# An 8-bit feed-forward block in a multi-stage kernel: the first map made feature-major, convolution taps applied behind it

## The chip, the cores and the metric

The kernel runs on one core of a Trainium2 chip. A core has five engines that run their own instruction streams: PE (TensorE, matrix products and transposes; "PEld" is its weight load), DVE (VectorE), ACT (ScalarE), POOL (GpSimd), and SP (SyncE), which here issues DMAs. The metric is the device time of one execution in microseconds (us). It is told as the median of several executions; one further execution is profiled, and all durations in the text come from that one.

## The reference

The reference is a long residual network over x, of shape (4, 512, 128): four layers, each with a cross attention and a feed-forward block. The change concerns the feed-forward block of the second layer, whose weights and inputs are rounded to few levels (a "bit linear" map):

```python
def act_quant(x):                       # per token, 8 bit
    scale = 127.0 / clip(max(abs(x), -1), 1e-5)
    return clip(round(x * scale), -128, 127) / scale

def weight_quant(w):                    # one scale per matrix, values -1, 0, 1
    scale = 1.0 / clip(mean(abs(w)), 1e-5)
    return clip(round(w * scale), -1, 1) / scale

h = bit_linear(x, w1)                   # (4, 512, 128) -> (4, 512, 512)
h = depthwise_conv1d(h, conv_w) + conv_b   # over tokens, 3 taps, zero padding, one filter per feature
h = silu(h)
x = x + bit_linear(h, w2)               # (4, 512, 512) -> (4, 512, 128)
```

The input x of the block is layer-normalized before. Written out for token t and feature f, the value in front of silu is c0[f] u[t-1, f] + c1[f] u[t, f] + c2[f] u[t+1, f] + b[f], where u is the first map's output and u outside of the row of 512 tokens is zero.

## The kernel before

**Stages.** The whole program is a sequence of stages. Most of them, and all that matter here, are written as a plan: pieces of work with the pieces they wait for, the buffers they take and use, and a planned cost on each engine that could do them (PE, V for DVE, S for ACT, G for POOL, Q for SP; costs in units of 10 ns). `Plan.run` (L191) is a list scheduler: it takes the ready piece that can start first, with the longest remaining path breaking ties, and issues it to the engine on which it would end first. The result is a fixed order of instructions on each engine; on the chip each engine runs its own order and waits in it. So an instruction that waits holds everything that stands behind it on its engine. PSUM has eight banks, which the plan hands out; buffers in SBUF come in rings of two or three.

The stages that the change touches, with their place in the profiled execution:

- *Expert stage of layer 0* (`first_part`, second plan, 176 to 322 us). Eight experts, one after the other: load the sorted tokens (`xe`, L1051), turn them, first map with silu (L1571 to L1578), second map (L1589), weighting on DVE (`ye`, L1134), and an indirect store per 128 tokens from POOL (L1020). Beside it, as filler, the plan prepares what later stages need: `bit_weights` (L1168) and `window_tables` (L1389), whose Exp runs at L1422.
- *Middle stage* (`middle_part`, 322 to 522 us). One plan holds the second layer's cross attention (`L686` to `L840`), the 8-bit block (`bit_ffn`, L1257), the third layer's window attention (L1439), and a normalization with a turn (L1614 to L1628) that hands the rows to the local transformer. All of it runs over four rows (batch entries b, 512 tokens each); the plan interleaves the rows. The rows' tensors x appear in the order of the program as x_79, x_81, x_83, x_85 for rows 0 to 3.
- *Local transformer* (522 to 2184 us), whose first weight loads SP issues at L1739.

**The 8-bit block.** For each row b: normalization (`norm`: moments on DVE at L536 and L538, 1/sigma on POOL at L546 and L547, then applied on DVE or POOL at L552); rounding to 8 bits by adding and subtracting a large constant (`scales` L1268 to L1271, `lift` L1278, `settle` L1283, either on DVE or POOL); four transposes (L1298) and a copy to `xqT`, the row with features on partitions and 512 tokens plus a zero column at either end (`ends`, L1292).

Then for each of the row's four token tiles (128 tokens): `hidden` (L1311) makes all 512 features of the tile in one PSUM bank by four products into one accumulation. A first one with a bfloat16 matrix of three rows adds the bias, and three fp32 products add one tap each; a tap is a shift of `xqT` by one column, with its own copy of the weights:

```python
t = hb.view(128, FF)
e.matmul(t, first[0:32], cb[0:32], start=True, stop=False)
for j in range(3):
    e.matmul(t, xqT.t[:, 128*tt + j : 128*tt + j + 128], w1T[:, j], start=False, stop=(j == 2))
```

The tile then has tokens on partitions. Silu is tanh on ACT (L1322) and one pass on DVE (L1325); the second rounding is per token (`scales` L1335 to L1338 on DVE, `inverse` L1341 on POOL, `lift` L1345 or L1347, `settle` L1352 or L1354); four bfloat16 transposes (L1364), a copy (`hqT`), the second map (L1371) and the residual add (L1377).

**The weights.** `bit_weights` loads w1, w2, the taps `cw` and the bias `cb`; rounds both matrices to -1, 0, 1 (`ternary`: L1206 to L1218); makes for each tap j a scaled copy of w1 (`tap`, L1232), turns it (L1236) and copies it to `w1T[:, j]`; and splits the bias, broadcast to all partitions, into three bfloat16 terms (`three_terms`, L316, called at L1195).

Of the kernel before, what the change touches and what calls it, by code (L numbers as in the profile page):

```python
# [239 lines left out]
def tile_kernel(ctx: ExitStack, tc: tile.TileContext, A: dict, out: bass.AP):  # L240
# [61 lines left out]
    def copy(e, dst, src):  # L302
        (e.copy if e is SC else e.tensor_copy)(dst, src)
# [864 lines left out]
    def bit_weights(plan, mp, wp):  # L1168

        w1, w2 = (wp.tile([128, NFC, 128], F32, name=f"bw{k}", bufs=1) for k in range(2))  # L1170
        cw = wp.tile([128, NFC, 3], F32, name="cw", bufs=1)
        cb = mp.tile([128, FF], BF16, name="cb")
        w1T = mp.tile([128, 3, FF], F32, name="w1T")
# [4 lines left out]
        row = plan.buf(wp, [128, FF], F32, "cbrow", 1)  # L1178

        def load(e):  # L1180
# [3 lines left out]
            e.dma_start(row.t, A["L1_ffn_conv_b"].partition_broadcast(128))  # L1184
# [5 lines left out]
        loaded = plan.add(load, takes=[row], Q=200)  # L1190
        done = [plan.add(magics, G=30, V=20)]
        for k in range(4):
            def terms(e, k=k):
                at = slice(128 * k, 128 * k + 128)
                three_terms(cb[:, at], row.t[:, at], wp, [128, 128], e)  # L1195

            done.append(plan.add(terms, [loaded], uses=[row], V=120))
# [27 lines left out]
        t1, t2 = ternary(w1, m1), ternary(w2, out_scale)  # L1225

        for j in range(3):
            bank, wj = plan.bank(), plan.buf(wp, [128, NFC, D], F32, "wj")

            def tap(e, j=j, wj=wj):  # L1230
                for c in range(NFC):
                    e.tensor_scalar(wj.t[:, c], w1[:, c], m1, cw[:, c, j : j + 1], ALU.mult, ALU.mult)  # L1232

            def flip(e, bank=bank, wj=wj):
                for c in range(NFC):
                    e.transpose(bank.view(128, NFC, 128)[:, c], wj.t[:, c], ident)  # L1236

            def out(e, j=j, bank=bank):
                copy(e, w1T[:, j], bank.view(128, FF))

            p = plan.add(tap, [t1], takes=[wj], V=112)
            p = plan.add(flip, [p], takes=[bank], uses=[wj], PE=54)
            done.append(plan.add(out, [p], uses=[bank], S=59, V=69))
# [11 lines left out]
        return done, w1T, w2T, cb, out_scale, magic  # L1255

    def bit_ffn(plan, wp, weights, start):  # L1257
        done, w1T, w2T, cb, out_scale, magic = weights
        last = []
        for b in range(B):  # L1260
# [29 lines left out]
            xqT, bank = plan.buf(wp, [128, S + 2], F32, "xqT"), plan.bank()  # L1290

            def ends(e, xqT=xqT):  # L1292
                e.memset(xqT.t[:, 0:1], 0.0)
                e.memset(xqT.t[:, S + 1 : S + 2], 0.0)
# [944 lines left out]
```

## Time and profile before

| | |
|---|---|
| median of three runs | 2434.31 us (2431.93 to 2436.33) |
| the profiled execution, its own time | 2475.2 us |
| its span in the profile | 2473.4 us |
| mean granted clock of PE | 0.956 |
| PE busy | 2242.8 us, 91% of the span |
| DVE busy | 1745.4 us, 71% |
| POOL busy | 1383.7 us, 56% |
| ACT busy | 1291.9 us, 52% |

Of the first map in the profile: the products with taps (L1315) are 96 records of 592 ns (an fp32 product leaves two), the bias products (L1313) 16 of 385 ns, the tanh (L1322) 16 of 597 ns, the pass behind it (L1325) 16 of 678 ns.

How to read the views that follow: the busy time by stretch gives, for a stretch of time, its length, the busy time of PE, PEld, DVE, ACT and POOL (with the number of instructions), the granted clock of PE as a share of full speed, and the load of the DMA engines. The chain of waits goes back from the last instruction, at each step to what released it; each of its lines has a start, the time that the chain spends there, the engine, the tensor written and the line. A timeline row has a start, a duration, the engine, the line, the operation, out<-in with shapes, and in brackets how long the engine was idle before it and what released it. Matmuls overlap: a record's duration is longer than the distance between two in a row, so sums over PE are made from the chain.

### The profile page before, as it was taken

The numbers are of one execution on the slowest core, as the hardware profiler recorded it, in microseconds if no ns is written. First come the engines' busy times: TensorE is split into PE (matmuls) and PEld (weight loads), VectorE is DVE, ScalarE is ACT, GpSimd is POOL, SyncE is SP. The second block draws the span as 40 slices with busy tenths as digits, with TensorE's granted clock in tenths as the row PEclk, the third lists the DMA queues.
The fourth block names the chain that finished last, engine by engine and source line by source line (L and its number), as shares of the span: only waits on it lengthen the run. The fifth ranks groups of instructions, "written<-read, shape, count | busy, mean of one in ns | idle before, by whom it ended". The sixth has DMA issues, their size and how long they took to land.

```text
span 2473.4 us, 86733 instructions
## 1 busy us (share of the span) xinstructions
PE 2242.8 (91%) x37341; PEld 1478.8 (60%) x37341; DVE 1745.4 (71%) x3818; ACT 1291.9 (52%) x2379; POOL 1383.7 (56%) x1948
## 2 busy tenths in 40 slices
PE   7959879968999999999999999999999999988686
PEld 3527644536666666666666666666666666644364
DVE  5626355757788888877887888888888888765522
ACT  3523225535666556666666666566666666533232
POOL 2242232446667666676667667766667666532433
PEclk9969989989999999999999999999999999989688
DMA  7210110015411121111211121111211111120022
GB/s 161 87 42 21 36 42 2 1 51 102 118 29 35 31 60 50 26 35 35 70 35 31 33 79 32 30 35 29 76 35 32 30 35 34 30 78 10 23 75 82
DMA packets 134297, 116.14 MB, mean 47 GB/s; under 512 B 29505, under 2 KB 102700, under 8 KB 133916
## 3 DMA queue, kind: packets, MB, share of 16 engines
q1 hardware_dynamic: 128373, 102.81, 16.0%
q0 software_dynamic: 4608, 7.35, 0.9%
q8 instruction: 296, 4.85, 0.8%
q14 instruction: 85, 0.70, 0.1%
q10 hardware_dynamic: 935, 0.43, 0.1%
HBM read 42.84 MB, written 21.52 MB: 26 GB/s over the span
## 4 chain that ended last, share of the span: by engine, by line
PE 71%; DVE 15%; issue 4%; DMA 3%; POOL 3%; ACT 2%; another core or an unknown queue 1%; SPq 1%; POOLq 0%; DVEq 0%; ACTq 0%
PE ps_tr L585 12%; PE ps_mm L1786 11%; PE ps_av L1948 6%; PE ps_av L1924 5%; PE ps_tr L1863 5%; PE ps_sc L1893 4%; DVE xn L523 3%; PE ps_sc L1994 2%; PE ps_sc L2006 2%; PE ps_sc L1983 2%; PE ps L776 2%; PE ps L1315 2%; PE ps L1687 2%; PE ps L785 2%; PE ps L1571 1%
## 5 line engine op out<-in xcount | busy, mean ns | idle before, releaser
L1809 POOL TENSOR_TENSOR rc<-rc,rs 128x512 f32<-128x512 f32 x384 | 489.8, 1276 | 382.7 <-DVE rs L1799 324.0
L1786 PE MATMUL ps_mm<-wqk,y 128*128 128x512 f32 x768 | 398.0, 601 | 10.4 <-DVE rs L1799 7.0
L1828 POOL TENSOR_TENSOR rc<-rc,rn_y 128x512 f32<-128x512 f32 x384 | 388.6, 1044 | 7.5
L1796 DVE TENSOR_TENSOR rc<-ps_mm,tabs 128x512 f32<-128x512 f32 x384 | 262.3, 683 | 139.1 <-ACT sq L1788 124.7
L1788 ACT ACTIVATE sq<-ps_mm 128x512 f32<-128x512 f32 x384 | 231.2, 603 | 167.0 <-PE ps_mm L1786 119.2
L1799 DVE TENSOR_TENSOR rs<-ps_mm,tabs 128x512 f32<-128x512 f32 x384 | 261.2, 680 | 0.3
L1808 DVE TENSOR_REDUCE ss<-sq 128x8 f32<-128x512 f32 x384 | 259.3, 675 | 0.0
L585 PE MATMUL ps_tr<-cst,rc 128*128 128x128 f32 x1536 | 211.7, 281 | 7.3 <-issue 4.1
L1924 PEld LDWEIGHTS ps_av<-v,PT 64*32 64x32 f32 x12288 | 138.4, 105 | 124.8 <-PE ps_tr L585 54.9
L1948 PE MATMUL ps_av<-aT,wo 128*128 128x128 f32 x1536 | 198.0, 281 | 4.3 <-issue 4.2
L1948 PEld LDWEIGHTS ps_av<-aT,wo 128*128 128x128 f32 x1536 | 179.5, 191 | 13.5 <-issue 4.6
L585 PEld LDWEIGHTS ps_tr<-cst,rc 128*128 128x128 f32 x1536 | 166.0, 142 | 27.9 <-issue 6.0
L1924 PE MATMUL ps_av<-v,PT 64*32 64x65 f32 x12288 | 170.3, 225 | 5.1 <-DVE attn L1934 1.1
L1893 PE MATMUL ps_sc<-kT,qT 64*32 64x64 f32 x12288 | 146.0, 224 | 25.3 <-issue 24.6
L1020 POOL DMA_INDIRECT back<-ye,to x80 | 78.0, 975 | 160.3 <-DVE ye L1134 117.7
L1786 PEld LDWEIGHTS ps_mm<-wqk,y 128*128 128x128 f32 x768 | 124.9, 193 | 60.5 <-issue 49.7
L1893 PEld LDWEIGHTS ps_sc<-kT,qT 64*32 64x32 f32 x12288 | 139.6, 105 | 35.1 <-issue 28.9
L766 ACT ACTIVATE P<-ps,deltaT 77x512 f32<-77x512 f32 x192 | 115.0, 684 | 69.2 <-PE ps L760 61.8
L1909 ACT ACTIVATE P<-P 128x1024 f32<-128x1024 f32 x96 | 101.5, 1057 | 90.9 <-DVE P L1904 90.9
L1820 ACT ACTIVATE rn_y<-ss 128x32 f32<-128x32 f32 x96 | 22.0, 229 | 236.6 <-POOL ss L1819 236.6
L1840 ACT COPY qT<-ps_tr 128x512 f32<-128x512 f32 x192 | 103.3, 589 | 75.4 <-PE ps_tr L585 75.1
L1840 ACT COPY kT<-ps_tr 128x512 f32<-128x512 f32 x192 | 103.4, 590 | 66.3 <-PE ps_tr L585 66.2
(410 smaller groups left out, 4414.3 us busy)
## 6 DMA issues: line engine op xcount, KB each, us to landing
v<-v SPq DMA_DIRECT2D x432, 65.0 KB
v<-v SPq DMA_DIRECT2D x96, 195.0 KB
wqk<-in_L_ffn_Wqkv_dram SPq DMA_DIRECT2D x24, 256.0 KB
sent<-xn SPq DMA_DIRECT2D x2, 2210.0 KB
xe<-sent SPq DMA_DIRECT2D x16, 260.0 KB
back<-xn SPq DMA_DIRECT2D x2, 2048.0 KB
raw<-in_L_ffn_W_dram SPq DMA_DIRECT2D x8, 512.0 KB
yb<-back SPq DMA_DIRECT2D x16, 256.0 KB
```

What stands on the lines that cost most here:

```text
L585: PE.transpose(t[:, i], src[:, i], ident)
L1786: PE.matmul(t, lhs, T.w[2 * kind + c], start=True, stop=True)
L1788: SC.activation(sq, t, AF.Square)
L1796: V.tensor_tensor(a, t, bc(T.tabs[:, 2 * kind, tt], [128, 8, LD], 1), ALU.mult)
L1799: V.tensor_tensor(r.rearrange("p h (x d) -> p h x d", x=2), t.rearrange("p h (x d) -> p h x d", x=2)[:, :, ::-1], bc(T.tabs[:, 2 * kind + ...
L1808: V.tensor_reduce(T.ss[:, kind, 8 * c : 8 * c + 8], sq, AX.X, ALU.add)
L1809: G.tensor_tensor(a, a, r, ALU.add)
L1828: G.tensor_tensor(a, a, bc(y[:, o : o + 8], [128, 8, LD], 2), ALU.mult)
L1840: SC.copy(t[:, 4 * c : 4 * c + 4, lead:], to_features(T.rot[kind, c].rearrange("p (k x) d -> p k (x d)", x=2)),)
L1893: PE.matmul(T.banks[32 * w : 32 * w + 32, z, k], T.qT[r, k, 32 * w : 32 * w + 32], T.kT[r, k, 32 * w : 32 * w + 64], start=False, stop=Tru ...
L1924: PE.matmul(T.means[32 * w : 32 * w + 32, x0, k], T.PT[r, 4 * g + k, 32 * w : 32 * w + 32], (T.v1 if w % 2 else T.v2)[r, x0, 4 * g + k], s ...
L1948: PE.matmul(t, T.wo[:, c], T.aT[:, c], start=(c == 0), stop=(c == 7))
```

## The change

In `bit_weights` the three scaled copies of w1 go, with their transposes, and one transposed copy of the rounded w1 takes their place (`flip1`, `out1`). The taps stay in a small tensor `cw` with features on partitions, multiplied once by the scale of w1 (`taps`). The bias is loaded with features on partitions, four values per partition, and isn't split any more.

In `bit_ffn` the first map runs with features on partitions: for each of four chunks of 128 features one product with all 512 tokens of the row (`product`). The result is read out of PSUM three times: once with the middle tap as scale and the bias as bias, on ACT (`own`, to `v`), and twice with an outer tap as scale, on ACT or DVE (`scaled`, to `n`). POOL adds the two neighbours in place, each one column out of step (`sides`); the missing neighbour at either end of the row is left out by the slices, so the zero columns of `xqT` and their memsets go. When all four chunks are done, `hidden` transposes the four chunks of a token tile into one PSUM bank, and all that follows is as before.

```diff
-        cw = wp.tile([128, NFC, 3], F32, name="cw", bufs=1)
-        cb = mp.tile([128, FF], BF16, name="cb")
-        w1T = mp.tile([128, 3, FF], F32, name="w1T")
+        cw = mp.tile([128, NFC, 3], F32, name="cw")
+        cb = mp.tile([128, NFC], F32, name="cb")
+        w1T = mp.tile([128, NFC, 128], F32, name="w1T")
...
-            e.dma_start(row.t, A["L1_ffn_conv_b"].partition_broadcast(128))
+            e.dma_start(cb, A["L1_ffn_conv_b"].rearrange("(c p) -> p c", p=128))
...
-        for k in range(4):
-            def terms(e, k=k):
-                at = slice(128 * k, 128 * k + 128)
-                three_terms(cb[:, at], row.t[:, at], wp, [128, 128], e)
-            done.append(plan.add(terms, [loaded], uses=[row], V=120))
...
-        for j in range(3):
-            bank, wj = plan.bank(), plan.buf(wp, [128, NFC, D], F32, "wj")
-            def tap(e, j=j, wj=wj):
-                for c in range(NFC):
-                    e.tensor_scalar(wj.t[:, c], w1[:, c], m1, cw[:, c, j : j + 1], ALU.mult, ALU.mult)
-            def flip(e, bank=bank, wj=wj):
-                for c in range(NFC):
-                    e.transpose(bank.view(128, NFC, 128)[:, c], wj.t[:, c], ident)
-            def out(e, j=j, bank=bank):
-                copy(e, w1T[:, j], bank.view(128, FF))
...
+        def taps(e):
+            e.tensor_scalar(cw, cw, m1, None, ALU.mult)
+        def flip1(e, bank=bank):
+            for c in range(NFC):
+                e.transpose(bank.view(128, NFC, 128)[:, c], w1[:, c], ident)
+        def out1(e, bank=bank):
+            copy(e, w1T, bank.view(128, NFC, 128))
...
-            xqT, bank = plan.buf(wp, [128, S + 2], F32, "xqT"), plan.bank()
-            def ends(e, xqT=xqT):
-                e.memset(xqT.t[:, 0:1], 0.0)
-                e.memset(xqT.t[:, S + 1 : S + 2], 0.0)
+            xqT, bank = plan.buf(wp, [128, S], F32, "xqT"), plan.bank()
...
+            v = plan.buf(wp, [128, NFC, S], F32, "bv")
+            mixed = []
+            for c in range(NFC):
+                ub, n = plan.bank(), plan.buf(wp, [128, 2, S], F32, "bn")
+                def product(e, c=c, ub=ub, xqT=xqT):
+                    e.matmul(ub.view(128, S), w1T[:, c], xqT.t, start=True, stop=True)
+                def own(e, c=c, ub=ub, v=v):
+                    e.activation(v.t[:, c], ub.view(128, S), AF.Identity,
+                                 scale=cw[:, c, 1:2], bias=cb[:, c : c + 1])
+                def scaled(e, c=c, ub=ub, n=n):
+                    for k in range(2):
+                        a, w = n.t[:, k], cw[:, c, 2 * k : 2 * k + 1]
+                        if e is SC:
+                            e.activation(a, ub.view(128, S), AF.Identity, scale=w)
+                        else:
+                            e.tensor_scalar(a, ub.view(128, S), w, None, ALU.mult)
+                def sides(e, c=c, n=n, v=v):
+                    d = v.t[:, c]
+                    e.tensor_tensor(d[:, 1:], d[:, 1:], n.t[:, 0, : S - 1], ALU.add)
+                    e.tensor_tensor(d[:, : S - 1], d[:, : S - 1], n.t[:, 1, 1:], ALU.add)
+                q = plan.add(product, [p] + done, takes=[ub], uses=[xqT], PE=88)
+                q = plan.add(own, [q], takes=[] if c else [v], uses=[ub] + ([v] if c else []), S=79)
+                r = plan.add(scaled, [q], takes=[n], uses=[ub], S=125, V=138)
+                mixed.append(plan.add(sides, [r], uses=[n, v], G=258))
...
-                    t = hb.view(128, FF)
-                    e.matmul(t, first[0:32], cb[0:32], start=True, stop=False)
-                    for j in range(3):
-                        e.matmul(t, xqT.t[:, 128 * tt + j : 128 * tt + j + 128], w1T[:, j],
-                                 start=False, stop=(j == 2))
+                    for c in range(NFC):
+                        e.transpose(hb.view(128, NFC, 128)[:, c],
+                                    v.t[:, c, 128 * tt : 128 * tt + 128], ident)
...
-                q = plan.add(hidden, [p] + done, takes=[hb], uses=[xqT], PE=285)
+                q = plan.add(hidden, mixed, takes=[hb], uses=[v], PE=58)
```

Since the plan decides the order, the new pieces and costs also move other pieces: in the middle stage rows 0 to 2 of the cross attention come earlier in PE's order than before, in the expert stage the loads of the window tables come ahead of the loads of the weights, and their Exp stands in the middle of an expert's silus instead of behind them.

## The prediction

> **What bounds the kernel now.** I read the page first (busy shares, slices), then the busy time by stretch around the changed stage, then the chain that ended last inside it, then the rows of single instructions. The change lies in two stages: the first expert stage (176 to 322 us), where the weights of the 8-bit block are prepared beside other work, and the middle stage (322 to 522), where the block runs between cross attention and window attention. The columns below are the stretch, its length, and busy time of PE, PEld, DVE, ACT and POOL, then PE's granted clock.
>
> ```profile
> 385.00:443.00 58.00, 57.66 (x730) 27.86 (x728) 32.69 (x92) 29.23 (x50) 16.86 (x32) 1.00 0.01 2
> 443.00:485.00 42.00, 41.69 (x188) 20.81 (x187) 30.48 (x104) 19.71 (x35) 18.42 (x34) 1.00 0.00 1
> 485.00:497.00 12.00, 9.08 (x79) 6.65 (x78) 11.08 (x47) 10.37 (x30) 3.60 (x8) 1.00 0.00 1
> 497.00:522.00 25.00, 17.15 (x102) 12.06 (x100) 17.59 (x79) 11.99 (x34) 7.66 (x11) 0.96 0.00 1
> ```
>
> From 385 to 485 PE is the bound, at full clock: 99.35 of 100 us. The other engines have room, POOL most. After 485 no engine is full; a chain of handoffs sets the pace. The chain shows what PE does:
>
> ```profile
> 442.73 0.32 PE ps L1313
> 443.05 2.77 PE ps L1315 x6
> 445.82 0.32 PE ps L1313
> 446.14 2.77 PE ps L1315 x6
> ...
> 519.89 1.26 PE ps L1618 x4
> 521.27 0.34 SPq L1739
> ```
>
> One token tile of the first map costs 0.32 (bias) + 2.77 (three taps) = 3.09 us, and sixteen of them 49.4 us. The last two lines say what the stage's end is worth: the weight loads of the next stage are issued right behind the last transposes of this one (SP's longest wait, 188.7 us, is for them). A microsecond saved at the end of the middle stage is therefore saved at the end of the kernel.
>
> **The middle stage, part by part.** PE: x6 in 2.77 us is three products, so one 128x512 product is 0.92 us; a row needs four, 16 x 0.92 = 14.8. Four fp32 transposes are 0.44 (the chain's L1298 x4), 16 x 0.44 = 7.1. PE falls from 49.4 to 21.9, **27.5 us less**. The two memsets (0.1 each) go for nothing.
>
> What comes in elsewhere:
> - ACT, `own`: 16. The trace has no such read with scale and bias pointers in this stage, but L1565 in the expert stage is the same form: 512 and 128 columns together take 1.13, so about 0.70 a piece: 11.2 us (0.60, as the tanh has, to 0.78, its full duration: 9.6 to 12.5).
> - `scaled`, 16 pairs, 10 on ACT and 6 on DVE by the order of the changed program: nearest rows are the tanh (0.60) and the copies out of PSUM on DVE (0.69); 1.3 us a pair: 13 and 8 us.
> - POOL, `sides`, 32 adds of 128x511. One row of this stage's timeline is the same kind, and a group of the page:
>
> ```profile
> 502.52 1.27 POOL L1510 TENSOR_TENSOR x<-x,wa_y 128x512 f32<-128x512 f32 x1 [1.19 <-ACT wa_y L1507]
> ```
>
> ```profile
> L1809 POOL TENSOR_TENSOR rc<-rc,rs 128x512 f32<-128x512 f32 x384 | 489.8, 1276 | 382.7 <-DVE rs L1799 324.0
> ```
>
> For comparison a pass of DVE over 512 columns, from the groups of 385 to 522 us:
>
> ```profile
> L1335 DVE TENSOR_REDUCE bh_m<-h 128x1 f32<-128x512 f32 x16 | 10.9, 681 | 3.6 <-POOL bh_s L1341 2.5 <-POOL xqT L1294 0.8
> ```
>
> So 1.28 each, 40.8 us. A rule of the Trainium skill speaks against this: "GPSIMD Engine Reference", section Engine selection, gives elementwise adds of two tensors to VectorE, GpSimd being about twice as slow. The trace agrees on the ratio (1.28 against 0.68). By the rule the 32 adds on DVE would be 22 us and a row's four chunks 5.4 instead of 10.2 us. But DVE has 63 of 100 us taken between 385 and 485, gets 8 more, and POOL had 35. In sum the row decides; on the path the rule is right, since each row waits for its own adds. In-place adds one column out of step occur nowhere in the trace: 1.28 to 1.9; I take 1.28.
>
> **What is on the path.** Total work no longer tells, so I lay the traced durations along the changed program's order on each engine. By that order, PE must do before row 3's output projection: 12 products (11.1), 8 token tiles (3.5), 12 turns and 24 small ones (2.6): 17.2 us. Before it was five tiles (15.5) and 1.1: 16.6. So **cross attention doesn't end earlier**: the projection stood at 441.6 and cannot start before 442.3. Then come the waits:
> - Row 1: its fourth product is ready at about 418.7. ACT then does own, three attention copies and tanh before the last `scaled`; the last add ends near 430.7. PE could turn row 1 at 427: 3.6 us lost.
> - Row 2: POOL does its last scaling in 3.1 us (L1282), ends 436.3, PE free at 434.7: 1.6 us lost, and 1 us for row 0's adds.
> - Queued behind these waits: on POOL all twelve chunks of rows 0 to 2 stand before row 3's 1/sigma (L546, L547; 1.3 us), which the whole rest of row 3 waits for; on ACT the Exp that PE's attention needs; on PE the attention of the next row.
>
> So row 3's projection comes near 448.6. Row 2's adds end at 453.7, 1/sigma 455.0, normalize 456.1, maxima behind a token tile's 458.6, POOL's lift 460.6, settle 461.7, turn 462.4, copy 463, first product 464.1, own 465.1, `scaled` 467.1, then four pairs of 2.56: 477.7 with a gap. Some twenty handoffs of 0.02 to 0.1 us (the chain's "issue" pieces) add 1.7: **479.4**. PE turned the last tile at 481.4 before, but spaced over 14 us; now four come at once. ACT must do 11.8 us from the first tanh to the last settle (tanh 0.60, lift 0.71, settle 0.7, copies 0.5, and row 2's Exp between), and turn, copy, down, residual take 2: last residual at 494.0 instead of 496.7. **2.7 us earlier.** Behind it came 24.4 us to the last transposes, of which some 4 were waits for rows 2's instructions on DVE and PE (the maxima of row 3 ran 1.5 us after PE was done, for example). Rows 0 to 2 are done sooner now: 2 us more. Middle stage: **-4.7**.
>
> **The expert stage.** Gone on DVE: four blocks of three_terms (each 1.9 us, at 206.4, 208.6, 211.0, 213.5, in between the ye products) and twelve tap scalings (0.34 each), on PE eight transposes, two copies. These ran under PE's matmuls and under POOL's scatter, with one exception: the first three scatters are issued 2.15 us apart because DVE brings ye late, where the rest come every 1.28. That is 1.7 us of a chain whose end (221.0) is when ACT goes on. Against it: the window's Exp now sits in the middle of expert 0's Silus, with two table loads of 1.28 and 0.46 of its own, 3.0 us, while ACT has 0.64 us idle in every 1.08. PE has eight banks to run ahead in, two per step, so I count 0.5 us; without the banks it would be 3. The loads: SP issues pt and leni first, so w1 comes 0.95 us later, needed only by weights used 200 us later. The bias is now a load of 512 four-byte pieces; cw with 512 pieces of 12 bytes was issued in 0.43 us. Nothing waits before 394. Sum: **-1.5** (-5 to +3).
>
> In all -6.2. The profiled execution took 2475.2 us (span 2473.4), 40.9 above the median of the runs (2434.3); from 2475.2 the sum makes 2469.0, and I carry the same difference over to the median: **2428**.
>
> **Rivals.**
> 1. *The freed PE shows.* If the waits above are covered, row 3 is projected at 442.7, and everything behind it comes 6 us sooner: -12; with another 3 each from the expert stage and a shorter tail, -18: 2416. For: DVE and ACT have room in the sum. Against: ACT rises from 29 to about 50 of 58 us between 385 and 443.
> 2. *Covered.* ACT's and POOL's queues cost 6 us more and the end stays where it was: 2430 to 2439.
> 3. *POOL becomes the bound: slower.* An add in place and one column off takes longer than 1.28, or DVE holds POOL up (the GpSimd page says that POOL shares its SBUF interfaces with VectorE). Of rows 2 and 3 eight pairs, 16 adds, lie in line on POOL before row 3 can be turned. Each 0.1 us more is 1.6 us; the gain is gone from 1.67 us per add on, and at 2.2 it is +9: 2443. For: POOL's own L1278 swings between 0.37 and 0.67. Against: L1809 holds 1.28 beside a busy DVE.
> 4. *The clock falls.* "TensorE: Matmul & The Clock Gate", Part 4, says transposes in PE mode don't count as busy for the gate. PE will be about half busy from 450 to 480, and mostly turning. By the rule, products and turns on row 3's path (about 4 us) double: +4. The row says: 485 to 497 had 9 of 12 us busy, nearly all transposes and small products, at 1.00, and it fell to 0.50 only when PE stood still past 520. I go by the row; the 4 us stay in the range.
>
> **Numbers.** Forecast (2421 to 2430) 0.37; rival 1 0.17; rival 2 0.22; rivals 3 and 4 together 0.24. No change means within 0.2% of the median, 4.9 us, about what a measurement of this kernel can tell. Half the chance on 2428 to 2430 goes to no change: faster 0.49, same 0.25, slower 0.26. Range 2411 to 2445: rival 1 below, an add of 2.2 us above, two in ten left out. The forecast's own range is 2421 to 2431.
>
> **What will show it.** PE's busy time 27 us lower; row 3's projection between 442 and 450; POOL's adds at 1.28 (above 1.67: rival 3); row 1's turn waiting for POOL some 4 us; the last residual near 494; the scatters of the first pair of experts evenly 1.28 apart; clock 1.00 from 450 to 500. I am wrong if PE stays unbroken through 443 (rival 1), or if the wait for POOL on PE's side sums to more than 15 us.

## The result, and the profile after

The changed kernel takes 2437.51 us (median of 14 runs, 2435.39 to 2445.04), the kernel before 2429.26 us beside it (14 runs, 2425.16 to 2436.33): ratio 1.0031, with a 95% interval of 1.0021 to 1.0042. It is **slower by 0.3%**, 7.5 us by the ratio and 8.3 by the medians. Forecast was 2428, faster by 6.2 than the 2434.3 that the kernel before was then taken to have. The profiled execution of the changed kernel took 2435.39 us (span 2433.6).

The first profile of the kernel before lies 46 us above its median, and in the last two series of experiments every kernel, the one before too, took some 40 us longer (by its third profile against its second 13 us ahead of the expert stage, 12 in it, 2 in the middle stage, 13 behind), so I compare middle stages, and times only as ratios to the kernel before on the same chip. Expert stage: from the first load of `xe` to the issue of the loads of `yb` (SP, L1155). Middle stage: from there to the first weight load behind the last turns (L1739 before, L1752 after).

| | expert stage | middle stage | of it, up to row 3's output projection (last start of L834) |
|---|---|---|---|
| before, first profile | 145.5 | 196.8 | 118.1 |
| before, profiled again | 132.2 | 197.0 | 118.2 |
| after, first profile | 129.5 | 206.4 | 130.7 |
| after, profiled again | 128.7 | 208.2 | 131.8 |

So the expert stage became 2.7 us shorter and the **middle stage 9.4 us longer**; together +6.7, which is the loss but for 1 to 2 us. Single profiles can't settle it more finely: behind the middle stage, where nothing was changed, the changed kernel's first profile is 7.0 us shorter than the second of before (1931.3 against 1938.3). The rest of the text is about the middle stage.

First the changed kernel's busy time by stretch, in the columns of the prediction. The four stretches follow the four shown before, counted from the issue of the loads of `yb` (28.5 us earlier here); the last is 10 us longer.

```profile
356.50:414.50 58.00, 52.58 (x583) 26.00 (x574) 45.21 (x112) 36.50 (x62) 27.61 (x33) 0.91 0.01 2
414.50:456.50 42.00, 31.30 (x274) 19.94 (x267) 31.83 (x97) 32.19 (x59) 29.56 (x37) 0.84 0.01 2
456.50:468.50 12.00, 8.17 (x63) 5.74 (x62) 11.31 (x41) 11.55 (x27) 4.80 (x9) 0.93 0.00 0
468.50:503.50 35.00, 26.07 (x132) 19.33 (x130) 20.68 (x90) 13.42 (x36) 12.61 (x18) 0.74 0.01 2
```

In the first 58 us PE was busy for 57.66 us and is now busy for 52.58; in the next 42 us it falls from 41.69 to 31.30. The work taken off PE shows. But the granted clock, 1.00, 1.00, 1.00 and 0.96 before, is 0.91, 0.84, 0.93 and 0.74, and DVE rose from 32.69 to 45.21 of 58 us.

How much of PE's saving went where can be added up. From 30 us after the start of the middle stage to 3 us before its end, in steps of 2 us, I sum PE's idle time and, as loss to the clock, busy time times (1 - granted clock). Before (profiled again): idle 10.1 us, lost to the clock 0.0. After: **idle 27.1, lost to the clock 16.8**. Of PE's saving of some 24 us (33.8 more idle or lost, less the 9.4 by which the stage grew), nothing arrived.

Next the chain that ended last in the changed kernel: start, time, engine, tensor, line.

```profile
366.86 2.98 DVE bx_n L552 x4
369.86 0.70 DVE bx_m L1258
...
371.07 1.62 DVE bn L1311 x3
372.69 0.36 issue
373.05 0.75 DVE bn L1311
373.85 0.37 PE ps L758
374.22 0.86 PE ps L760 x8
375.08 1.78 PE ps L776 x32
376.86 1.71 PE ps L785 x8
...
419.36 1.29 POOL bv L1315
...
428.08 1.09 POOL bv L1316
...
481.49 1.93 PE ps L1472 x8
...
500.97 1.27 PE ps L1631 x4
502.29 0.35 SPq L1752
```

The four DVE passes that normalize row 1 (L552) take 2.98 us where four took 1.1. Behind them DVE reads the scaled copies out of PSUM (L1311), only then is a bank free for PE's next attention piece (L758), and from 375 on the products run at half speed: L776 x32 takes 1.78 us, at full clock 1.01. Near the end L1472 x8 takes 1.93 us (1.0 at full clock). The last two lines still hold: the weight loads wait for the last turns.

The groups of the first map in the changed kernel (busy us and mean ns behind the bar):

```profile
L1315 POOL TENSOR_TENSOR bv<-bv,bn 128x511 f32<-128x511 f32 x16 | 20.5, 1278 | 8.6 <-ACT bn L1309 7.8 <-DVE bn L1311 0.8
...
L1316 POOL TENSOR_TENSOR bv<-bv,bn 128x511 f32<-128x511 f32 x16 | 17.5, 1094 | 1.3
L1298 PE MATMUL ps<-xqT,w1T 128*128 128x512 f32 x32 | 16.7, 644 | 0.1
...
L1329 PE MATMUL ps<-cst,bv 128*128 128x128 f32 x64 | 9.3, 298 | 0.0
```

POOL's additions take 1.28 and 1.09 us, 38.0 in all, less than the 40.8 of the forecast. The whole new PE work, products and turns, is 26.0 us by records, which overlap.

### The profile page after: what moved, and what is told of

It reads as the page before. It is cut to its first block, busy times and chain, and to the rows that moved or that the text cites. A ratio compares the mean times of both kernels' runs of the same rounds, so it can differ in the third digit from the quotient of the medians.

```text
span 2433.6 us, 86722 instructions
## 1 busy us (share of the span) xinstructions
PE 2210.9 (91%) x37317; PEld 1476.4 (61%) x37317; DVE 1752.2 (72%) x3800; ACT 1314.9 (54%) x2419; POOL 1405.5 (58%) x1957
## 4 chain that ended last, share of the span: by engine, by line
PE 71%; DVE 14%; issue 4%; POOL 4%; DMA 3%; ACT 3%; SPq 1%; POOLq 0%; ACTq 0%; DVEq 0%
PE ps_tr L585 13%; PE ps_mm L1799 11%; PE ps_av L1961 6%; PE ps_av L1937 5%; PE ps_tr L1876 5%; PE ps_sc L1906 5%; PE ps_sc L2007 2%; PE ps_sc L1996 2%; PE ps_sc L2019 2%; DVE xn L523 2%; PE ps L776 2%; PE ps L785 1%; PE ps L1700 1%; PE ps L1585 1%; PE ps L1584 1%
## 5 line engine op out<-in xcount | busy, mean ns | idle before, releaser
L1799 PE MATMUL ps_mm<-wqk,y 128*128 128x512 f32 x768 | 396.8, 599 | 10.8 <-DVE rs L1812 7.6
L1947 DVE TENSOR_TENSOR attn<-ps_av,la_den 128x512 f32<-128x512 f32 x192 | 132.8, 692 | 6.6
```

The costliest lines, as they stand in the source:

```text
L1799: PE.matmul(t, lhs, T.w[2 * kind + c], start=True, stop=True)
```

## The experiments

The theories: **POOL** (the additions, by their own time on the rows' path and by holding DVE up), **clock** (PE's granted clock falls in the gaps that the change opens), **order** (DVE's and ACT's queues and the handoffs alone). In the table, projection, idle and clock loss are measured as above, in one profile each; ratios are to the kernel before on the same chip. The middle stage of the kernel before was 196.8, 197.0 and 198.6 us in its three profiles, so stages can be compared to about 2 us. A run that changes costs or pieces of the plan changes the order of other pieces too.

| run | what it is | ratio to before, 95% interval | middle stage | up to row 3's projection | PE idle | lost to clock |
|---|---|---|---|---|---|---|
| after_again | the change | 1.0016 (1.0002 to 1.0029) | 208.2 | 131.8 | 24.6 | 24.6 |
| sides_tiny | additions cut to 8 columns | 0.9994 (0.9980 to 1.0009) | 198.7 | 125.0 | 21.1 | 18.0 |
| fill_row0 | useless products in row 0 | 1.0039 (1.0025 to 1.0053) | 201.7 | 125.7 | 24.6 | 11.8 |
| fill_turn0 | useless transposes in row 0 | 0.9996 (0.9978 to 1.0014) | 206.2 | 129.9 | 23.0 | 18.3 |
| sides_dve | additions on DVE | 1.0052 (1.0036 to 1.0068) | 214.9 | 123.5 | 28.2 | 23.6 |
| norm_act | normalization on ACT | 1.0017 (0.9996 to 1.0039) | 203.7 | 124.9 | 22.7 | 18.4 |
| fused | taps by DVE from PSUM | 1.0014 (1.0002 to 1.0026) | 202.4 | 116.9 | 24.0 | 16.7 |
| fused_fill | the same, useless products | 1.0044 (1.0031 to 1.0057) | 202.8 | 117.2 | 23.1 | 11.7 |
| pool01 | the change for rows 0, 1 | 1.0037 (1.0022 to 1.0051) | 204.0 | 131.2 | 17.6 | 13.6 |
| pool23 | the change for rows 2, 3 | 1.0017 (0.9998 to 1.0036) | 200.7 | 124.7 | 17.6 | 9.8 |
| hybrid01 | taps by DVE, rows 0, 1 | 0.9983 (0.9970 to 0.9996) | 192.4 | 121.2 | 12.3 | 3.2 |
| hybrid01_more | hybrid01 again | 0.9994 (0.9973 to 1.0014) | 189.6 | 119.2 | 11.4 | 3.2 |
| hybrid01_v1 | hybrid01, one buffer for v | 0.9993 (0.9974 to 1.0012) | 196.7 | 124.5 | 12.2 | 8.3 |
| hybrid012 | taps by DVE, rows 0 to 2 | 1.0002 (0.9986 to 1.0018) | 193.2 | 123.3 | 16.1 | 7.5 |

### Both kernels once more

> The kernel before, unchanged, profiled once more, since the first profile of it lies 46 us above its median. Expected: an own time of 2425 to 2436 us; the stretch from the issue of the loads of yb (the start of the middle stage) to the first weight load behind the last transposes within 2 us of the 196.8 us of the first profile if the middle stage of that profile was undisturbed, and the expert stage (from the first xe load to the issue of the loads of yb) near 129 to 132 us rather than 145.5. If the middle stage comes out 8 us or more shorter than in the first profile, then the changed kernel loses still more there than the two profiles say.

> The changed kernel, unchanged, on the chip of the other experiments, so that its stages can be set beside theirs. Expected: ratio to the kernel before 1.002 to 1.004 again; the middle stage (from the issue of the loads of yb to the first weight load behind the last transposes) 205 to 208 us against 197.0 in the second profile of the kernel before; PE's granted clock near 0.5 for some 11 us behind the wait after row 0's products. If the middle stage comes out at 200 or less, the 206.4 us of the first profile were chance and the loss lies elsewhere.

> The kernel before once more, one look: middle stage 196.5 to 197.5 us on this chip too; if it differs by more than 1 us, stages can't be compared across chips.

The kernel before took 2436.6 us in its second profile, with a middle stage of 197.0 and an expert stage of 132.2: the excess of the first profile lay outside the middle stage. The third, 198.6, is 1.1 us more than was allowed for, hence the 2 us above. The changed kernel's ratio, 1.0016, is a little below what was expected, its stage, 208.2, just above the upper edge, and the half clock behind row 0's products lasted 17 us there (372 to 389) instead of 10.

The third profile also bears on the clock. In front of the transposes of L1364 PE waits once for 1.1 to 1.2 us (at 492.4 in the first profile of the kernel before, at 493.2 in the third). The stretch with most of that wait and the next one, first profile:

```profile
492.50:495.90 3.40, 2.29 (x21) 2.11 (x22) 3.31 (x18) 2.04 (x6) 1.67 (x3) 1.00 0.00 0
495.90:499.30 3.40, 3.17 (x22) 2.03 (x20) 2.91 (x17) 2.25 (x4) 0.65 (x2) 1.00 0.00 0
```

Third profile:

```profile
490.60:494.00 3.40, 2.21 (x14) 0.97 (x14) 3.23 (x19) 3.40 (x13) 0.63 (x3) 1.00 0.01 2
494.00:497.40 3.40, 3.04 (x16) 2.92 (x17) 2.67 (x11) 1.36 (x3) 1.56 (x3) 0.50 0.00 0
```

PE stood idle for 1.1 us in the one and 1.2 in the other; the clock held in the one and fell to 0.50 in the other, in the same kernel. The stretches are cut where the clock can change: in each of the 18 profiles all its falls and rises lie on one grid with steps of 3.41 us, whatever PE is doing. In the first profile of the change it falls at 375.1, 436.6, 446.8, 467.3, 481.0 and 498.0, which is 18, 3, 6, 4 and 5 steps apart.

### The additions left out

Of each addition only 8 columns are left, so most of the neighbours are missing in the sum.

```diff
-                    e.tensor_tensor(d[:, 1:], d[:, 1:], n.t[:, 0, : S - 1], ALU.add)
-                    e.tensor_tensor(d[:, : S - 1], d[:, : S - 1], n.t[:, 1, 1:], ALU.add)
+                    e.tensor_tensor(d[:, 1:9], d[:, 1:9], n.t[:, 0, :8], ALU.add)
+                    e.tensor_tensor(d[:, :8], d[:, :8], n.t[:, 1, 1:9], ALU.add)
```

> The changed kernel with each of POOL's 32 additions cut from 511 columns to 8 (so most of the neighbours are left out of the sum); the order of every engine is the same, only POOL is free. Theory POOL (the additions cost, by their own time on the rows' path and by holding up DVE's passes from SBUF to SBUF, which took 2.7 to 3.0 us for four beside an addition and 1.1 without): DVE's four passes of the normalization (L552) take 1.1 us in all rows, PE no longer stands at 371 to 374, and the time falls by 8 us or more, to 2430 or less, not slower than the kernel before. Theory clock (TensorE's granted clock falls whenever it waits between the first map's steps): waits remain for ACT and DVE, the clock still falls to 0.5 somewhere between 374 and 494, and the time falls by at most 5 us. Theory order (handoffs and queues of ACT and DVE alone): within 2 us of 2437.5.

The middle stage is 198.7 us, 7.7 to 9.5 less than with the additions, and the time is that of the kernel before. One row of the trace says why DVE is part of it: the normalizing passes of the 8-bit rows, with minimum, median and maximum in ns. The changed kernel:

```profile
L552 DVE TENSOR_SCALAR bx_n<-x,bx_mv,bx_rs x16: 335/342/1289, 346.6 to 431.4; 128x128 f32<-128x128 f32 x16
```

The same kernel, same order on every engine, with the small additions:

```profile
L552 DVE TENSOR_SCALAR bx_n<-x,bx_mv,bx_rs x16: 339/342/352, 348.3 to 428.8; 128x128 f32<-128x128 f32 x16
```

The longest pass falls from 1289 to 352 ns. A pass that meets an addition stands still for its length. So POOL's theory holds for the greater part of the loss. But the run doesn't part its two halves: the additions' own time goes as well, and 10 us of it stand in the chain of the changed kernel (L1315 and L1316, 419.4 to 429.6), where the forecast had priced it. Nor is the clock's theory refuted: 18.0 us are still lost to the clock here, and the stage is still 1.7 us longer than before.

### Useless products in the gap

```diff
-                    e.matmul(ub.view(128, S), w1T[:, c], xqT.t, start=True, stop=True)
+                    for _ in range(1 + (b == 0)): e.matmul(ub.view(128, S), w1T[:, c], xqT.t, start=True, stop=True)
```

> The changed kernel with the four products of row 0's first map done twice into the same bank: 3.7 us of useless work more on PE, put in front of the wait of 2.1 us behind which PE's granted clock fell to 0.50 for 11 us (375 to 386). Theory clock: PE no longer stands long at 371 to 374, the granted clock stays 1.00 there, which is worth some 5.5 us, and row 3's output projection comes 2 to 4 us earlier in spite of the added work; time 2432 to 2437. Theories POOL and order: the added work is in line on PE, the projection comes 1.6 to 3.7 us later, time 2438 to 2442.

Busy time by stretch around the gap, first the changed kernel:

```profile
366.00:370.00 4.00, 4.00 (x48) 1.72 (x47) 3.11 (x5) 4.00 (x8) 3.15 (x3) 1.00 0.00 0
370.00:374.00 4.00, 1.90 (x27) 0.53 (x20) 3.69 (x8) 2.64 (x5) 2.66 (x5) 1.00 0.00 0
374.00:378.00 4.00, 4.00 (x49) 2.03 (x46) 2.85 (x5) 2.40 (x4) 3.90 (x5) 0.64 0.02 6
378.00:382.00 4.00, 4.00 (x52) 2.35 (x52) 2.86 (x6) 0.00 (x0) 2.09 (x2) 0.50 0.00 0
382.00:386.00 4.00, 4.00 (x24) 0.93 (x17) 0.00 (x0) 0.23 (x1) 0.00 (x0) 0.58 0.00 0
```

The same stretches with the four useless products:

```profile
366.00:370.00 4.00, 4.00 (x11) 1.65 (x9) 3.86 (x9) 3.49 (x6) 2.04 (x2) 1.00 0.00 0
370.00:374.00 4.00, 4.00 (x61) 1.82 (x64) 2.69 (x5) 2.32 (x5) 3.75 (x7) 1.00 0.00 0
374.00:378.00 4.00, 4.00 (x84) 1.98 (x80) 3.14 (x5) 3.16 (x6) 3.84 (x6) 1.00 0.03 6
378.00:382.00 4.00, 3.99 (x48) 1.85 (x37) 2.86 (x7) 0.82 (x2) 1.09 (x1) 1.00 0.00 0
382.00:386.00 4.00, 3.59 (x59) 1.98 (x57) 2.44 (x6) 2.55 (x5) 0.00 (x0) 1.00 0.02 4
```

PE's 2.1 us of idle time at 370 to 374 are filled, and the clock that fell to 0.50 stays at 1.00, though DVE is still held up (longest pass 1283 ns). Row 3's projection comes 5.0 us earlier, the stage is 4.7 us shorter, with 3.7 us more work on PE. In the stage, then, a lower clock was worth about 5 us at this one place (one profile each). The time doesn't follow: 2446.95 us, ratio 1.0039, where the stages of the profile say +1.2 us. In that profile the untouched local transformer took 6.0 us longer than in that of the kernel before. Why the unchanged stages took longer stays open, so I use this run for the stage alone.

> The changed kernel with eight useless turns of 128x128 (0.11 us each at full clock, 0.88 in all) in front of each of row 0's four products, in place of the useless products of the other run: the same time of PE, at the same place, by transposes. If only the idle gap counts (the wait at 371 to 374 is filled): granted clock 1.00 from 374 to 386 as with the products, middle stage 200 to 204 us. If transposes don't count as busy for the clock gate, as the page on the clock gate says: the granted clock still falls to 0.5 somewhere between 370 and 390, and the middle stage is 206 to 212 us.

```diff
+                    for k in range(8 if b == 0 else 0):
+                        at = slice(128 * (k % 4), 128 * (k % 4) + 128)
+                        e.transpose(ub.view(128, S)[:, at], xqT.t[:, at], ident)
                     e.matmul(ub.view(128, S), w1T[:, c], xqT.t, start=True, stop=True)
```

With transposes as filling the clock stayed at 1.00 at that place too (1.00 from 395 to 416, the whole run being 21 us later there): not what the Trainium skill's "TensorE: Matmul & The Clock Gate", Part 4, leads one to expect of transposes. It is a weak test, since each eight transposes were followed by a real product. The clock then fell at 420.4, behind gaps of 0.6, 0.2 and 0.6 us within 3 us, and the stage was 206.2 us: inconclusive as to the time.

### The additions on DVE

`sides` is planned with V=136 instead of G=258.

> The changed kernel with the 32 neighbour additions given to DVE in place of POOL (0.68 us a pass by the row of the maxima: 22 us more on DVE, 40 less on POOL). Theory POOL: nothing holds up DVE's passes from SBUF to SBUF any more, a row's four chunks take 5.4 instead of 9.5 us, and the middle stage is 199 to 203 us. Theory clock with order: DVE, already 4.9 of 6 us busy between 390 and 450, becomes the bound, PE waits more and its clock falls more often: middle stage 207 to 214 us.

214.9 us, the longest stage of all. The rule that the prediction weighed (two-tensor additions belong on VectorE) was right on the rows' path: the projection comes 7 to 8 us earlier. Behind it DVE has everything to do, and 91.4 us pass to the end instead of 75.7.

### Taps by DVE straight out of PSUM

```diff
-                r = plan.add(scaled, [q], takes=[n], uses=[ub], S=125, V=138)
-                mixed.append(plan.add(sides, [r], uses=[n, v], G=258))
+                mixed.append(plan.add(taps2, [q], uses=[ub, v], V=130))
...
+                def taps2(e, c=c, ub=ub, v=v):
+                    d, u = v.t[:, c], ub.view(128, S)
+                    e.scalar_tensor_tensor(d[:, 1:], u[:, : S - 1], cw[:, c, 0:1], d[:, 1:], ALU.mult, ALU.add)
+                    e.scalar_tensor_tensor(d[:, : S - 1], u[:, 1:], cw[:, c, 2:3], d[:, : S - 1], ALU.mult, ALU.add)
```

> The changed kernel with the neighbours added by DVE straight out of PSUM: two passes per chunk, each tap times the shifted product plus the sum, in place of the two scaled copies (ACT or DVE) and POOL's two additions. POOL loses 37 us, ACT 12.6, DVE gains 32 x 0.62 = 19.8 less the 8.5 of its scaled copies. Theory POOL: the chunk's path shortens from 0.7 + 1.3 + 2.4 to 0.7 + 1.3 us and nothing holds DVE's normalization up; row 3's projection comes 5 us or more earlier and the time is 2424 to 2431, at or below the kernel before. Theory order (DVE and ACT in order set the pace): DVE has 11 us more and the time is 2436 to 2445. Theory clock: the granted clock below 1.00 still accounts for several us between 440 and 494 of the stage, time 2430 to 2436.

The time is a miss: ratio 1.0014, where the theory of POOL asked for the kernel before or less. Up to the projection this is what the change could have been: 116.9 us, 13.8 less than the change and 1.3 less than before. Behind it 85.5 us pass instead of 78.8. Three stretches of it:

```profile
404.00:416.00 12.00, 11.74 (x117) 7.00 (x116) 11.59 (x30) 10.11 (x17) 5.10 (x11) 1.00 0.01 2
416.00:434.00 18.00, 12.04 (x60) 7.57 (x59) 17.24 (x48) 13.03 (x21) 8.11 (x15) 0.72 0.00 1
434.00:458.00 24.00, 16.40 (x98) 12.22 (x96) 22.14 (x70) 16.65 (x34) 12.57 (x20) 0.69 0.00 1
```

DVE is busy for 51.0 of 54 us, so the bound is now DVE, and PE's clock falls beside it. Which of the two decides was tried with useless products in front of the eight turns of rows 2 and 3 (which also keeps `xqT` in use for longer):

```diff
                 def hidden(e, b=b, tt=tt, hb=hb, v=v, xqT=xqT):
+                    for _ in range(1 if b > 1 else 0):
+                        e.matmul(hb.view(128, S), w1T[:, 0], xqT.t, start=True, stop=True)
                     for c in range(NFC):
...
-                q = plan.add(hidden, mixed, takes=[hb], uses=[v], PE=58)
+                q = plan.add(hidden, mixed, takes=[hb], uses=[v, xqT], PE=58)
```

> The kernel with the taps applied by DVE straight out of PSUM, and in front of each of the eight turns of rows 2 and 3 one useless product of 128x512 (0.92 us at full clock) into the bank that the turn then overwrites: 7.4 us of work more on PE, between 415 and 455, where the granted clock fell to 0.5 (the stage was 202.4 us without it). Theory clock: the granted clock stays at 1.00 for most of 420 to 470, and the middle stage is 196 to 200 us in spite of the added work. If the clock doesn't matter (DVE and the handoffs decide): 203 to 209 us, since each useless product stands in front of a turn that was awaited.

The last of the three stretches with them:

```profile
434.00:458.00 24.00, 17.93 (x116) 11.30 (x114) 21.59 (x66) 15.96 (x33) 12.57 (x21) 1.00 0.01 1
```

The clock is 1.00 where it was 0.69, and the stage is the same length (202.8, just below the 203 to 209 that was expected if the clock doesn't matter). That DVE decides here and not the clock is likely, as DVE is busy for 21.6 of 24 us with the full clock too. It isn't shown: each useless product stands in front of an awaited turn, and what that costs may hide a gain from the clock. (The time, ratio 1.0044, again lies above what the stages say, as in the other run with useless products.)

### The normalization off DVE

```diff
+        def scaled_by_act(e):
+            for t in range(NT):
+                e.activation(dst.t[:, t], x[b][:, t], AF.Identity, scale=rs.t[:, t : t + 1], bias=nb.t[:, t : t + 1])
...
-            p = norm(plan, b, start[b], xn, "bx")
+            p = norm(plan, b, start[b], xn, "bx", act=True)
```

> The changed kernel with the normalization of the 8-bit block's rows applied by ACT (four passes of scale and bias; POOL makes the bias, 0.5 us more there) in place of DVE; POOL's additions stay as they are. Theory hold-up: DVE no longer stands still beside the additions before row 1, PE's wait behind row 0's products and the half clock after it go, and the middle stage is 198 to 204 us. Theory POOL's own time: the additions come no sooner, ACT gets 4 x 1 us more, stage 206 to 211 us.

203.7 us, 2.7 and 4.5 less than the two profiles of the change, with the additions in place: in the span that was expected of the hold-up, though not far beyond what profiles of one kernel differ by. The clock is 1.00 from 392 to 422, the place of the fall (22 us later in this run), and falls at 422.6. The time (1.0017) tells nothing apart.

### The new map for some rows only

These kernels are the kernel before with both sets of weights, and the new map for rows 0 and 1, or 2 and 3, or 0 to 2. `pool01` and `pool23` make it as the change does, with one buffer for `v`; the hybrids with the taps on DVE.

```diff
+            fm = b in (0, 1)
...
-                q = plan.add(hidden, [p] + done, takes=[hb], uses=[xqT], PE=285)
+                if fm:
+                    q = plan.add(turned_back, mixed, takes=[hb], uses=[v], PE=58)
+                else:
+                    q = plan.add(hidden, [p] + done, takes=[hb], uses=[xqT], PE=285)
```

> The kernel before, with the first map of rows 0 and 1 made exactly as the change does (scaled copies by ACT or DVE, additions by POOL), rows 2 and 3 as before; only one buffer for v instead of two, since both sets of weights stand in SBUF. If POOL's additions and DVE's hold-ups cost wherever they stand, the middle stage is 197 to 203 us. If the change is harmless while PE has cross attention to do, and the loss belongs to rows 2 and 3, where nothing else keeps PE busy: granted clock 1.00 up to 455, stage 190 to 195 us, about the 192.4 of the version with taps on DVE.

> The complement: rows 0 and 1 as before, rows 2 and 3 as the change does it, with one buffer for v. If the loss belongs to the rows behind cross attention: granted clock below 1.00 from about 440 on, middle stage 203 to 212 us. If it comes from rows 0 and 1 (the wait behind row 0's products and the half clock after it): 195 to 199 us.

Rows 0 and 1 alone lose 7.0 us, 1 us more than the span of the hold-up; rows 2 and 3 alone lose 3.7, between the two spans that were expected (either with the single buffer). That the change is harmless beside cross attention is refuted. The timeline of the first shows the hold-up at its clearest. On DVE (start, time, operation, and in brackets the idle time before it):

```profile
399.47 4.76 DVE L552 TENSOR_SCALAR bx_n<-x,bx_mv,bx_rs 128x128 f32<-128x128 f32 x4
404.15 0.73 DVE L740 SCALAR_TENSOR_TENSOR shift<-high,cst,ps 128x512 bf16<-128x512 bf16 x1
```

On POOL at the same time:

```profile
399.34 1.26 POOL L1353 TENSOR_TENSOR bv<-bv,bn 128x511 f32<-128x511 f32 x1
400.68 1.09 POOL L1354 TENSOR_TENSOR bv<-bv,bn 128x511 f32<-128x511 f32 x1
401.72 1.26 POOL L1353 TENSOR_TENSOR bv<-bv,bn 128x511 f32<-128x511 f32 x1
403.06 1.09 POOL L1354 TENSOR_TENSOR bv<-bv,bn 128x511 f32<-128x511 f32 x1
```

And on PE:

```profile
404.94 0.65 PE L758 MATMUL ps<-shift,pick 32*77 32x512 bf16 x4 [4.96 <-DVE shift L740]
```

Two chunks' additions stand back to back on POOL. Four passes of 0.34 us take 4.76: each gets through between two additions. `shift` (L740), which has nothing to do with the 8-bit block, stands behind them on DVE, PE's attention waits 4.96 us for it, and runs at half clock from 403.2 to 423.6.

> The kernel before, with rows 0 and 1 of the 8-bit block by the new map (taps applied by DVE out of PSUM) and rows 2 and 3 by the old one (three products per tile). Rows 0 and 1 run beside cross attention, where PE is full, and save 2 x (12.4 - 3.7 - 1.8) = 13.8 us of PE there; rows 2 and 3 keep PE full to the end of the map, without additions to wait for. Theory clock: the granted clock stays 1.00 up to 480 and the middle stage is 188 to 194 us, against 197.0 before; time 2427 to 2434 where the kernel before has 2437 (ratio 0.996 to 0.999). If PE's load was not what set the end of the stage, or waits take its place: 196 to 200 us, ratio 1.000 to 1.003.

> The version with rows 0 and 1 by the new map and taps on DVE, with one buffer for v as the run with POOL's additions had. If the single buffer made the difference of 11.6 us between the two: middle stage 200 to 206 us. If POOL's additions did: 191 to 196 us.

> The version with rows 0 and 1 by the new map and taps on DVE, timed again: ratio to the kernel before 0.997 to 0.9995, middle stage 191.5 to 193.5 us. If its gain was chance: ratio 1.000 or above.

> As the version with rows 0 and 1 by the new map and taps on DVE (middle stage 192.4 us), but row 2 too: 6.9 us less PE work, of which the last tiles lie behind cross attention. If PE's load still sets the end there: 186 to 191 us. If row 2's tiles were what kept the clock up between 420 and 460: the granted clock falls there, and the stage is 193 to 200 us.

With the taps on DVE the same two rows gain. Busy time by stretch of hybrid01:

```profile
360.00:418.00 58.00, 55.54 (x710) 27.89 (x704) 43.14 (x110) 34.82 (x58) 11.08 (x27) 1.00 0.01 2
418.00:460.00 42.00, 39.56 (x217) 21.50 (x214) 37.00 (x137) 32.45 (x68) 15.21 (x31) 1.00 0.00 1
460.00:472.00 12.00, 11.10 (x73) 9.18 (x74) 9.95 (x46) 6.93 (x20) 5.39 (x8) 0.86 0.01 2
472.00:492.00 20.00, 12.24 (x61) 8.89 (x60) 11.48 (x51) 8.01 (x20) 3.88 (x7) 0.80 0.00 0
```

PE is busy for 95.1 of 100 us at clock 1.00 up to 460, with 13.8 us less to do by the sum, and the stage is 192.4 and 189.6 us in two profiles: 4.6 to 7.4 less than the 197.0 of before. In time it is **faster than both kernels** in one series, by little, 0.9983 (0.9970 to 0.9996), and not told apart from the kernel before in the other, 0.9994 (0.9973 to 1.0014). One buffer for `v` costs 4.3 to 7.1 us of that (196.7), so the fair comparison of the additions by POOL with the taps on DVE is 204.0 against 196.7: 7.3 us. With row 2 as well (193.2) the clock falls from 455 to 465 and nothing more is gained.

## Why the prediction was wrong, point by point

- **What bounds the kernel: right.** PE was full at full clock up to row 3's map; taking work off it there does shorten the stage (hybrid01).
- **The work: right in size, nearly.** Products 16.7 us of records (forecast 14.8 along the chain), additions 38.0 (40.8), `own` 0.79 and `scaled` 1.26 a pair, on DVE 1.41 (1.3). Rival 3's addition of 1.67 us or more is refuted; so is rival 1, since PE is broken from 370 on. The measured 2437.5 lies in the range of rival 2, by luck: there the end of the stage stays where it was, here it comes 9.4 us later, with the expert stage hiding a part.
- **The expert stage: right.** Forecast -1.5 (its two terms, -1.7 and +0.5, make -1.2); 2.7 and 3.5 shorter than in the second profile of before, and the scatters of the first experts are 1.28 us apart from the first one on, instead of 2.15.
- **Row 3's projection: too early.** Forecast 124.2 us into the stage, measured 130.7 and 131.8. The steps had the passes on DVE at the durations of the kernel before (row 3's normalization as 1.1 us, from the end of 1/sigma to the end of normalize). That row held where it was read, but beside an addition the passes take up to 1289 ns each. I had asked what holds POOL up ("DVE holds POOL up", in rival 3) and not the reverse: the hold-up of DVE, the second step that failed, stands at nothing in the sum. Out of the hold-up come the 2.1 us of PE's wait for L1311 behind row 0's products, which the forecast doesn't have; the waits for POOL that it does have (3.6, 1.6 and 1 us) shrink to 1.0 us on PE, for row 2's turn (L1284).
- **The clock: the step that failed.** The prediction put it so: "the row says: 485 to 497 had 9 of 12 us busy [...] at 1.00, and it fell to 0.50 only when PE stood still past 520. I go by the row". So the sum has nothing for the clock. The row was one profile's luck: in the third profile of the same kernel the clock fell at that place for 3.4 us. (In the first it fell at 519.8, behind a wait of 3.3 us, not past 520.) The change makes gaps of 2 us and more, in pieces, and 3 to 17 us at half clock follow on each. Read along the chain of the changed kernel: six attention pieces between 375 and 386 are 4.6 us longer than at full clock (9.74 against some 5.1), 4.3 us of pieces between 451 and 456 twice their due (2.2), and 8 us of pieces between 481 and 491 twice their due (4.0). That would be 10.8 of the 14.1 us by which the middle stage was misjudged (-4.7 against +9.4). It is an estimate and an upper one, since a shorter piece may uncover another wait; only the first part was tried (5.0 us, fill_row0). Rival 4 had the mechanism at +4, on row 3's path alone. By the rule that I set aside ("TensorE: Matmul & The Clock Gate", Part 4) the forecast would have been 2432, nearer in number, but the rule's reason isn't borne out here: with transposes in the gap the clock held (fill_turn0, a weak test).
- **Behind the projection: too short.** Forecast 68.0 us; 75.7 and 76.4. Row 3's last residual stands at 176.8 us into the stage, forecast 169.5, and 29.6 us follow, 24.6 before. Of the 7.7 us too many, 4.0 are the half clock of 481 to 491 and 2.2 that of 451 to 456, by the estimate above; for the rest POOL's last normalization (L552, 3.38 us for four) and full queues on DVE are in the chain, and no run isolates them.

What is shown: with the additions gone most of the loss goes (sides_tiny); at one place the fall of the clock costs the stage some 5 us with the additions and hold-ups in place (fill_row0); taking DVE's pass out of the way removes that gap with the additions in place, for 2.7 to 4.5 us (norm_act). The shares overlap and don't add up to one sum: the additions hold DVE up, DVE leaves PE without a bank, PE's clock falls. How much the falls behind 440 cost, and why most of them come with the additions gone as well, stays open.

## What to carry to other kernels

Work taken off a full engine is worth something only if that engine stays full: here 24 us less work became 17 us of gaps and 17 us of lower clock, so price the gaps with the stretch at half clock behind them, not by their length alone, and don't take one profile at full clock for a rule. Before giving POOL additions between tensors in SBUF, look for DVE's passes from SBUF to SBUF in the same stretch, and at what is queued behind them. Where stages differ in their bound, make the exchange only for the part in which the relieved engine is full: with the taps on DVE, the new map in two rows brought the stage from 197.0 to 192.4 and 189.6 us, in all four to 202.4.

## What the runs showed of the hardware that I had not expected

- DVE's pass over 128 columns stands still for the whole of POOL's addition: 0.34 us alone, 1.29 at most beside one, 4.76 for four beside four additions. The Trainium skill's "SBUF — State Buffer", section SBUF: two separate sides, calls the ports that the two share an exclusive lock held for the whole instruction; this trace agrees, and it was mostly DVE that lost (the longest addition took 1.45 us, the median of its line 1.27). DVE's reads from PSUM (L1311, 1.41 us a pair beside additions and without) were not held.
- The granted clock fell behind broken gaps: 2.1 us idle within 2.5 (the change, 375.1), 1.4 within 3 (fill_turn0, 420.4), while single gaps of 1.34 us in the kernel before passed. "TensorE: Matmul & The Clock Gate", Why this matters for your kernels, asks only for no idle gaps above some 3 us; here shorter ones did it. Counted on the grid of 3.41 us, from 25 us into the middle stage, in all 18 profiles: steps at full clock in which PE was idle for less than 0.66 us all kept it (592), steps with more than 1.99 us all lost it (31), and of those between 97 kept and 47 lost it. So idle time alone doesn't decide; what else does was not tried.
- All 75 stretches at half clock in these stages lasted 1 to 6 whole steps: 10.2 us in the first profile of the change (375.1 to 385.4), 17.1 in the second, 20.5 in pool01, with PE shown busy nearly all through: attention products with 32 or 77 rows. Where whole products of 128 rows and 512 columns followed, it lasted one step (the change, 436.6 to 440.0). Rows alone don't explain it: from 481.0 to 491.2 it was three steps too, mostly with products and transposes of 128 rows.
